# Turning on TensorE instead of by DMA, and another order in the last block of a fused transformer kernel

## The chip, the core and the metric

The kernel runs on one core of one Trainium2 chip. The metric is the device time of one execution in microseconds (us); the time before is the median of three runs, 1993.96 us (1993.28 to 1995.19). The engines of a core work side by side and meet through semaphores: TensorE (PE in the profile, with its weight loads listed as PEld), VectorE (DVE), ScalarE (ACT), GpSimd (POOL), and SyncE (SP), which issues most DMAs.

## The reference

For two sequences of 2048 tokens with 512 channels the reference computes, in float32, an attention-like block and then a feed-forward part, each added to its input:

```python
x = x + attn(cond(x, cond_512, ...), ...)     # modulated linear layer, gated linear recurrence, gated MLP
x = x + ffn(cond2(x, tokens, ...), rhs)       # the part that the change touches
```

The second line is the stage at hand. With `_ln` a layer norm over the 512 channels whose gain and shift are looked up by token class:

```python
h = _ln(x, pw_g[pathway_ids], pw_b[pathway_ids]);  h = _ln(h, cp_g[compartment_ids], cp_b[compartment_ids])
t = _ln(x, tm_g[time_steps], tm_b[time_steps]);    s = _ln(x, ms_g[scale_type], ms_b[scale_type])
m, n, r = (x + state_vector for each of three conditions)        # one vector per sequence
cat = concat([w[0]*h, w[1]*t, w[2]*m, w[3]*n, w[4]*r, w[5]*s])   # 6 x 512 channels
y = _ln(silu(cat @ int_W1 + int_b1) @ int_W2 + int_b2, int_g, int_be)
# ffn: int8-style product
q = clip(round(y / scale_y), -127, 127);  out = (q @ q_rhs) * scale_y * scale_rhs
```

`scale_y` is the largest absolute value of a token's row divided by 127, `scale_rhs` the same by column of `rhs`.

## The kernel before

**Tiling.** The first 1360 us (modulated layer, recurrence, MLP) are not touched by the change. The last stage works on 8 blocks of T = 512 tokens, 4 blocks per sequence. Within a block the channels lie on the partitions for the products, and the tokens lie on the partitions for the norms, so data must be turned between the two layouts.

**The big product.** After the terms that share `x` are merged, `cat @ int_W1` is four 512-channel operands (x, t, s, h) times a weight with 512 outputs. `up` does it with seven products in place of eight: `paired_in_place` splits operands and outputs into halves (B11, B21 are the first 256 tokens of the first and second pair of operands, B12, B22 the last 256) and runs the steps a (slot 0, B11), b (slot 1, B21), d (slot 6, B22), d (slot 4), a (slot 5), e (slot 2), a (slot 3). Each step is 16 fp32 matrix products, which the profile lists as 32 passes (L134); the letters are PSUM banks, and in the profile the tiles ps_h_a, ps_h_b, ps_h_d and ps_h_e. `tap` copies or combines what later steps need (L1576 on; L1582 is its ACT copy, tap 5 is called `less`, tap 3 is k3), `sums` forms differences of the operands in place (L222), `out11`, `out12`, `out22` and `out21` add up a quarter of the output and apply silu (L1600 to L1615), and `added` adds the parts that depend on a token's class alone by a short bf16 product with `tables` and `z2T` (L1594). `then` is a dictionary of functions that are traced after step n, or, with the key (n, u), after half u of it.

**The next block's norms.** While block i is in its steps, `by_tokens` for block i+1 turns x by TensorE (`tr_x`, L1458), takes statistics on VectorE (L1348), forms the normed rows `ln` (L1362), and prepares `z1`: one-hot rows times the norm's factors, in bf16. The turned `z1T` is the moving operand of the class gains (`gains`, L1551). `branch_by_tokens` gathers the rows of `pw` by POOL's indirect DMA (L1390), multiplies and adds them (L1502, L1503) for two pairs of token tiles, and takes the statistics of the first pair. `rows_by_tokens`, placed behind k3, takes those of the second pair and forms `z2`; its turned `z2T` serves the third gain and `added`. `branch_by_channels` turns h0 by TensorE (`tr_h`, L1371), and ACT copies it out (L1374).

**Turning by DMA.** `to_rows` (L1438) turns z1 and z2 with a transposing DMA on SP; `int8_values` (L1685) does it with the int8 values of the block before. In the first block half of z2 is turned by TensorE already (`rows_of_first`, L1529).

**The rest of a block.** `down2` multiplies by `w2` (L1633, ps_o) with the next block's gains in between, adds the bias and takes statistics. Norm, scales and int8 values of block i-1 (`last_norm`, `int8_values`) run on VectorE during block i, and `int8_product` (L1657, ps_f) on TensorE behind the product steps; VectorE scales it (L1660), adds x and SP stores it.

**The last block** has no successor. `part_norm` does the w2 product of one tile of 128 tokens, with the bias as an fp32 product of a row of ones (L1705, L1707), the norm (L1642, L1643), the scale (L1646, L1649) and the rounding (L1652); `part_product` turns by TensorE (L1725), copies on VectorE (L1727), multiplies (L1657) and stores. Tiles 2 and 3 are normed in the middle of the last step a, tiles 0 and 1 after it, and then all four products follow.

**Order of the work.** A tile framework orders each engine's instructions: by the order in which they are traced, but an instruction whose operands it estimates to be late is overtaken by later ones. `tc.issue_after(ins)` keeps what is traced in it behind `ins` on the same engine; `tc.manual_schedule` keeps the traced order (TensorE in the first block's first steps). On the chip each engine then takes its instructions in that fixed order.

**PSUM.** `m2_ps` has four buffers of one bank for products. `tr` hands out two buffers in turn (`turn[0] ^= 1`) to every turn and gain.

## Time and profile before

| what | value |
|---|---|
| time, median of 3 runs | 1993.96 us (1993.28 to 1995.19) |
| profiled execution: time, span | 1991.8 us, 1990.0 us |
| TensorE busy in the span | 1972.5 us (99%) |
| VectorE, ACT, POOL busy | 1180.4, 658.4, 146.4 us |
| granted TensorE clock, mean | 0.997 |
| last stage: one steady block | 73.03 to 73.04 us |
| last block: start to the end of its last w2 product | 1901.50 to 1973.03 us |
| from there to the end of the span | 16.97 us |

A row of a timeline gives start, duration, engine, line, operation, tiles (output <- inputs) and count; a bracket tells how long the engine stood idle before it and what released it. Tiles that share memory carry the name of the place (zone_A, zone_B, zone_C and the like): q0 is in zone_A, z1T in zone_C, and pw is the second pair's buffer. fp32 matrix products appear as two passes each. The chain of waits is followed back from the end; a row in it gives start, duration, engine, tile and line. A table of stretches gives, per engine, the busy time and number of instructions within each stretch.

### The profile page before, as it was taken

The page shows a single profiled execution, that of the slowest core. Times are in us where ns is not written, and L with a number is a line of the kernel's source. Part 1 is how long each engine was busy: PE and PEld are TensorE (multiplying, and loading weights), DVE is VectorE, ACT ScalarE, POOL GpSimd, SP SyncE. Part 2 cuts the span into 40 slices and gives each one's busy share as a digit, 9 for nine tenths or more (in the row PEclk, how much of TensorE's full clock was granted, in tenths as well). Part 3 has the DMA queues.
Part 4 walks back from the last instruction along what each step waited for, and adds up shares of the span by engine and source line. Part 5 has one row for each costly group of instructions (what it writes and reads, how often), then busy time and mean ns, then how long its engine had stood idle before and what let it go on. Part 6 is the DMA issues. An engine that isn't in the chain of part 4 may idle for free.

```text
span 1990.0 us, 16593 instructions
## 1 busy us (share of the span) xinstructions
PE 1972.5 (99%) x6060; PEld 1054.8 (53%) x6068; DVE 1180.4 (59%) x1907; ACT 658.4 (33%) x889; POOL 146.4 (7%) x123
## 2 busy tenths in 40 slices
PE   9999999999999999999999999999999999999997
PEld 5444444444444444444444444444867867877774
DVE  6667666666633324324224564646788888788775
ACT  4557777777522222222221100001213213212302
POOL 0241000000400000000010000025000000000000
PEclk9999999999999999999999999999999999999999
DMA  6661212121511212111335666453322222222110
GB/s 220 204 201 53 89 59 95 53 95 43 159 47 66 89 42 82 56 42 53 101 100 170 209 232 235 156 170 127 121 69 85 59 72 82 65 73 74 43 32 22
DMA packets 115774, 201.36 MB, mean 101 GB/s; under 512 B 37728, under 2 KB 66034, under 8 KB 111596
## 3 DMA queue, kind: packets, MB, share of 16 engines
q1 hardware_dynamic: 111028, 183.49, 28.2%
q0 software_dynamic: 4608, 16.78, 2.4%
q8 instruction: 48, 0.79, 0.2%
q14 instruction: 34, 0.28, 0.0%
q10 hardware_dynamic: 56, 0.03, 0.0%
HBM read 133.59 MB, written 58.83 MB: 97 GB/s over the span
## 4 chain that ended last, share of the span: by engine, by line
PE 93%; DVE 5%; ACT 0%; DMA 0%; issue 0%; SPq 0%; DVEq 0%
PE up_a L134 17%; PE rec_a L134 11%; PE dn_a L134 8%; PE up_d L134 8%; PE ps_h_a L134 6%; PE ps_h_d L134 6%; PE rec_d L134 6%; PE ps_o L1633 5%; PE dn_d L134 4%; PE up_b L134 4%; PE ps_h_b L134 3%; PE y_a L134 3%; PE rec_b L134 3%; PE dn_b L134 2%; PE y_d L134 1%; PE ps_f L1657 1%
## 5 line engine op out<-in xcount | busy, mean ns | idle before, releaser
L134 PE MATMUL up_a<-h,w_up 128*128 128x512 f32 x384 | 172.6, 592 | 0.0
L134 PE MATMUL dn_a<-op,w_dn 128*128 128x512 f32 x384 | 168.9, 599 | 0.0
L821 DVE SCALAR_TENSOR_TENSOR prod<-up_d,cols,k 128x512 f32<-128x512 f32 x48 | 36.0, 750 | 199.5 <-ACT k L304 199.5
L304 ACT COPY k<-up_a 128x512 f32<-128x512 f32 x144 | 84.0, 584 | 196.8 <-PE up_a L134 196.7
L801 ACT ACTIVATE gate<-gate,cols 128x512 f32<-128x512 f32 x96 | 68.8, 721 | 215.3 <-DVE gate L800 214.2
L134 PE MATMUL up_a<-h2T,w_up 128*128 128x512 f32 x288 | 129.5, 593 | 0.0
L134 PEld LDWEIGHTS up_a<-h,w_up 128*128 128x128 f32 x384 | 73.1, 190 | 91.7 <-issue 89.3
L134 PEld LDWEIGHTS dn_a<-op,w_dn 128*128 128x128 f32 x384 | 73.0, 192 | 90.2 <-issue 89.7
L134 PE MATMUL rec_a<-h,w_rec 128*128 128x512 f32 x256 | 115.1, 592 | 0.0
L134 PE MATMUL rec_a<-hT,w_rec 128*128 128x512 f32 x256 | 115.1, 592 | 0.0
L1633 PE MATMUL ps_o<-int_w,h 128*128 128x512 f32 x224 | 103.6, 606 | 0.0
L134 PEld LDWEIGHTS up_a<-h2T,w_up 128*128 128x128 f32 x288 | 54.8, 190 | 68.8 <-issue 68.8
L134 PE MATMUL up_b<-h,w_up 128*128 128x512 f32 x192 | 86.3, 592 | 0.0
L134 PE MATMUL up_d<-h,w_up 128*128 128x512 f32 x192 | 86.3, 593 | 0.0
L134 PE MATMUL dn_d<-op,w_dn 128*128 128x512 f32 x192 | 83.7, 594 | 0.0
L134 PEld LDWEIGHTS rec_a<-hT,w_rec 128*128 128x128 f32 x256 | 48.7, 190 | 61.2 <-issue 61.2
L134 PEld LDWEIGHTS rec_a<-h,w_rec 128*128 128x128 f32 x256 | 48.7, 190 | 61.2 <-issue 60.7
L304 ACT COPY k<-rec_a 128x512 f32<-128x512 f32 x96 | 55.6, 579 | 71.5 <-PE rec_a L134 70.0
L800 DVE TENSOR_TENSOR gate<-up_b,k 128x512 f32<-128x512 f32 x48 | 32.9, 690 | 72.1 <-PE up_b L134 71.0
L134 PE MATMUL up_d<-h2T,w_up 128*128 128x512 f32 x144 | 65.2, 593 | 0.0
L1633 PEld LDWEIGHTS ps_o<-int_w,h 128*128 128x128 f32 x224 | 40.3, 190 | 46.5 <-issue 46.5
L222 DVE TENSOR_TENSOR op<-op,op 128x3072 f32<-128x3072 f32 x16 | 55.2, 3448 | 16.2 <-PE dn_d L134 9.3
(408 smaller groups left out, 3403.2 us busy)
## 6 DMA issues: line engine op xcount, KB each, us to landing
pp_d<-prod SPq DMA_DIRECT2D x48, 512.0 KB
op<-pp_d SPq DMA_DIRECT2D x16, 1536.0 KB
y_d<-y SPq DMA_DIRECT2D x16, 512.0 KB
h<-y_d SPq DMA_DIRECT2D x4, 2048.0 KB
yr<-y_d SPq DMA_DIRECT2D x16, 512.0 KB
hs_d<-yr SPq DMA_DIRECT2D x16, 512.0 KB
h<-hs_d SPq DMA_DIRECT2D x4, 2048.0 KB
op<-in_xT SPq DMA_DIRECT2D x32, 256.0 KB
```

Of the source, the lines that this page charges most:

```text
L134: ins = nc.tensor.matmul(ps, ws[k // 2][:, slot, k % 2, ts(u, P)], xs[k], start=(first and k == 0), stop=(last and k == n - 1), skip_group ...
L222: nc.vector.tensor_sub(t, p, q)
L304: nc.scalar.copy(t, ps)
L800: nc.vector.tensor_add(gate[u][:, half], ps, kept)
L801: nc.scalar.activation(gate[u][:, half], gate[u][:, half], AF.Gelu, bias=col("L0_attn_mlp_gate_b", fs[u]),)
L821: nc.vector.scalar_tensor_tensor(prod[u][:, b_], ps, col("L0_attn_mlp_fc_b", fs[u]), kept, ALU.add, ALU.add)
L1633: nc.tensor.matmul(ps, h1[:, c, ts(j, P)], w2[:, c, :], start=(c == 0), stop=(c == C - 1))
L1657: nc.tensor.matmul(ps, qT[:, ts(c, P)], rq[:, c, :], start=(c == 0), stop=(c == C - 1))
```

## The change

1. **Turns.** `to_rows` no longer issues a DMA: it turns tile by tile with TensorE into a PSUM tile, and ACT copies the result out. It is called for z1 after step a (slot 5) of the block before (`then[4]`), and for z2 in `down2` behind the w2 product of tile 2. The int8 values get a function of their own, `int8_rows`, called in the middle of step n = 2 (d with slot 6, in the last block d with slot 4) and after it. In the first block both halves of z2 go through `rows_of_first`.
2. **Second pair.** The product and sum of the second pair of `branch_by_tokens` become a function `pair`, called behind `less` (`then[5]`).
3. **Last block.** With `by_tiles`, step b (B21, slot 1) comes after step e, and the last step (slot 3) is done by two tiles of 128 tokens, each followed by its sums and silu. The w2 products of tiles 2 and 3 stand in and after step b; the product of tile 2 and the w2 product of tile 0 follow the first token tile, and the others the second.
4. **Bias.** The bias row of the last block is split into three bf16 rows (`ones_b2`), made by POOL and three small DMAs at the start of the stage, and added by one bf16 product with three rows of ones.
5. **Rounding.** In the last block ACT subtracts the rounding constant, and both limits are applied where the turned tile is copied.

```diff
...
             k3 = tap(3, pa, kd)
         more(3, pd)
         out22(pd, k3)
+        if by_tiles:
+            kept = tap(7, pe, k2)
+            pb = banks("b")
+            step(pb, 1, B21, True, not added)
+            sums(B21, B21, B22)
+            c11()
+            by_tiles([x[:, k, :] for x in B21 for k in range(x.shape[1])], 3, kept)
...
+            return
         kept = [tap(6, pe, None)] if shared else []
         step(pa, 3, B21, False, not added)
         more(4, pa)
...
+    ones_b2 = io.tile([P, P + D], BF, name="ones_b2")[0:3]
+    nc.gpsimd.memset(ones_b2[:, 0:P], 1.0)
+    t = place("qT0", D)[0:1]
+    h = place("qT1", 2, D, dtype=BF)
+    nc.gpsimd.tensor_copy(t, b2_bc[0:1])
+    for n in range(3):
+        part_of = h[0:1, n % 2, :]
+        nc.gpsimd.tensor_copy(part_of, t)
+        if n < 2:
+            nc.gpsimd.tensor_sub(t, t, part_of)
+        nc.sync.dma_start(ones_b2[n : n + 1, P:], part_of)
+    less_magic = small.tile([P, 1], FP, name="less_magic", bufs=1)
+    nc.gpsimd.memset(less_magic, -MAGIC)
...
-    def to_rows(dst, src):
-        nc.sync.dma_start(
-            dst.rearrange("p a (j t) -> p (a j) t", t=P),
-            src.rearrange("p a j t -> p (a j t)"), transpose=True,
-        )
+    def to_rows(dst, src, pt):
+        for n in range(dst.shape[1]):
+            for j in range(J):
+                nc.tensor.transpose(pt[:, n, ts(j, P)], src[:, n, j, :], identb)
+        nc.scalar.copy(dst, pt)
...
         k["z1T"] = place("z1T", 2, T, dtype=BF)
-        to_rows(k["z1T"], z1)
...
                 gather(i * J + 2 * q + j, pw[:, j, :])
+        def pair(q):
             nc.vector.tensor_mul(h0[q], ln[q], h0[q])
-            nc.vector.tensor_add(h0[q], h0[q], pw[:, :, D : 2 * D])
-            if not q:
-                pair_stats(0)
+            nc.vector.tensor_add(h0[q], h0[q], place(f"pw{q}", 2, 2 * D)[:, :, D : 2 * D])
+        pair(0)
+        pair_stats(0)
+        k["pair"] = pair
         k["rest"] = z2, of_means, mv2, pair_stats
...
         k["z2T"] = place(f"z2T{i % 2}", 2, T, dtype=BF)
-        if i:
-            to_rows(k["z2T"], z2)
-        else:
-            k["z2"] = z2
-            to_rows(k["z2T"][:, 1:2], z2[:, 1:2])
+        k["z2"] = z2
         return last
-    def rows_of_first():
-        pt = m2_ps.tile([P, D], BF, tag="mm", name="tr_z2")
-        for j in range(J):
-            nc.tensor.transpose(pt[:, ts(j, P)], k["z2"][:, 0, j, :], identb)
-        nc.scalar.copy(k["z2T"][:, 0, :], pt)
+    def rows_of_first(n):
+        pt = m2_ps.tile([P, 1, D], BF, tag="mm", name=f"tr_z2_0_{n}")
+        to_rows(k["z2T"][:, n : n + 1], k["z2"][:, n : n + 1], pt)
+    def rows_of(n, i, k):
+        to_rows(k[f"z{n}T"], k[f"z{n}"], tr(f"tr_z{n}_{i}", BF))
     def by_tokens(i, k):
         norm_by_tokens(i, k)
...
         def tap(n, ps, less):
-            t = place(f"k{ {1: 0, 4: 1, 2: 2, 5: 1, 3: 1, 6: 2}[n]}", 2, H)
+            t = place(f"k{ {1: 0, 4: 1, 2: 2, 5: 1, 3: 1, 6: 2, 7: 2}[n]}", 2, H)
             if n == 5:
-                nc.vector.tensor_sub(t, ps, less)
+                held["less"] = nc.vector.tensor_sub(t, ps, less)
+            elif n == 7:
+                nc.vector.tensor_add(t, both(ps), less)
             elif n == 3:
                 held["k3"] = nc.vector.tensor_add(t, both(ps), less)
...
+            if by_tiles:
+                for o in (0, 1):
+                    silu(o, h_a, h1[:, o, h_a])
         def out12(ps, kept):
             nc.vector.tensor_add(h1[:, 0:2, h_b], both(ps), kept)
             for o in (0, 1):
-                silu(o, slice(0, T), h1[:, o, :])
+                half = h_b if by_tiles else slice(0, T)
+                silu(o, half, h1[:, o, half])
         def out22(ps, kept):
             nc.vector.tensor_add(h1[:, 2:4, h_b], both(ps), kept)
...
+        def last_by_tiles(X, slot, kept):
+            for j in (0, 1):
+                part = ts(j, P)
+                ps = [x[:, 0:P] for x in banks(f"t{j}")]
+                for u in (0, 1):
+                    product(ps[u], w_int, slot, [x[:, part] for x in X], u, not u, False)
+                added(4, ps, part)
+                for u in (0, 1):
+                    h = h1[:, 2 + u, part]
+                    nc.vector.tensor_add(h, ps[u], kept[:, u, part])
+                    silu(2 + u, part, h)
+                then["tile", j]()
+        by_tiles = last_by_tiles if i == NB - 1 else None
         paired_in_place(
             w_int, *([t[:, :, h] for t in q] for h in (h_a, h_b) for q in (first, second)),
...
                 for c in range(C):
-                    nc.tensor.matmul(
+                    ins = nc.tensor.matmul(
                         ps, h1[:, c, ts(j, P)], w2[:, c, :], start=(c == 0), stop=(c == C - 1)
                     )
+                if nxt and j == 2:
+                    with tc.issue_after(ins.ins):
+                        rows_of(2, i + 1, nxt)
                 t = o4[q][:, j % 2, :]
                 nc.vector.tensor_add(t, ps, b2_bc)
                 stats(mv, j, t, f"s3_{i}")
...
         nc.vector.tensor_scalar(qn, qn, -127.0, None, ALU.max)
-        nc.sync.dma_start(
-            place(f"qT{q}", 2, D, dtype=BF).rearrange("p j (c t) -> p (j c) t", t=P),
-            qn.rearrange("p j d -> p (j d)"), transpose=True,
-        )
+    def int8_rows(i, q, behind):
+        qn, pt = place(f"q{q}", 2, D, dtype=BF), tr(f"trq_{i}_{q}", BF)
+        with tc.issue_after(behind.ins):
+            for j in (0, 1):
+                for c in range(C):
+                    nc.tensor.transpose(pt[:, j, ts(c, P)], qn[:, j, ts(c, P)], identb)
+        nc.scalar.copy(place(f"qT{q}", 2, D, dtype=BF), pt)
     def int8_product(i, qs, x2n, q, behind):
...
         ps = m2_ps.tile([P, D], FP, tag="mm", name=f"ps_o_{i}_{j}")
-        nc.tensor.matmul(ps, ones[0:1, :], b2_bc[0:1, :], start=True, stop=False)
+        nc.tensor.matmul(ps, ones_b2[:, 0:P], ones_b2[:, P:], start=True, stop=False)
         for c in range(C):
...
         qn = places["pw0"].bitcast(BF)[:, ts(j, D)]
-        rounded(qn, t)
+        nc.scalar.activation(qn, t, AF.Identity, bias=less_magic)
         return t, qs, qn
     def part_product(i, j, t, qs, qn):
...
         qT = places["pw1"].bitcast(BF)[:, ts(j, D)]
-        nc.vector.tensor_scalar(qT, pt, -127.0, None, ALU.max)
+        nc.vector.tensor_scalar(qT, pt, 127.0, -127.0, ALU.min, ALU.max)
         by_rhs(t, qT, qs[:, 1, :], f"ps_f_{i}_{j}")
...
         norm_by_tokens(0, k, (ends[4], mids[5]))
+        rows_of(1, 0, k)
         branch_by_tokens(0, k)
+        k["pair"](1)
         branch_rows = rows_by_tokens(0, k)
...
         (0, 0, 1): times,
-        (0, 1, 1): rows_of_first,
+        (0, 1, 1): lambda: rows_of_first(0),
+        (1, 1, 0): lambda: rows_of_first(1),
         (1, 0, 0): lambda: gains(0, k, 2),
         1: first_block.close,
     }
-    def behind_k3(i, k):
-        with tc.issue_after(held["k3"].ins):
-            rows_by_tokens(i, k)
+    def behind(name, f, *args):
+        with tc.issue_after(held[name].ins):
...
             then[1] = lambda: [int8_values(i - 1, qs[0], q) for q in PAIRS]
-            then[2] = lambda: int8_product(i - 1, qs[0], last["x2n"], 0, held["ins"])
+            then[2, 0] = lambda: int8_rows(i - 1, 0, held["ins"])
+            then[2] = lambda: (
+                int8_rows(i - 1, 1, held["ins"]),
+                int8_product(i - 1, qs[0], last["x2n"], 0, held["ins"]),
+            )
             then[3, 0] = lambda: int8_product(i - 1, qs[0], last["x2n"], 1, held["ins"])
         if nxt:
             then[3] = lambda: by_tokens(i + 1, nxt)
-            then[6, 0] = lambda: behind_k3(i + 1, nxt)
+            then[5] = lambda: behind("less", nxt["pair"], 1)
+            then[6, 0] = lambda: behind("k3", rows_by_tokens, i + 1, nxt)
+            then[4] = lambda: behind("ins", rows_of, 1, i + 1, nxt)
             then[6] = lambda: branch_by_channels(i + 1, nxt)
         else:
             parts = {}
-            def half():
-                for j in (2, 3):
-                    parts[j] = part_norm(i, j)
-            then[6, 0] = half
+            def part(j):
+                parts[j] = part_norm(i, j)
+            def product_of(j):
+                part_product(i, j, *parts[j])
+            then[5, 0] = lambda: part(2)
+            then[5] = lambda: part(3)
+            then["tile", 0] = steps((product_of, 2), (part, 0))
+            then["tile", 1] = steps((product_of, 3), (part, 1), (product_of, 0), (product_of, 1))
         up(i, k, then)
         if nxt:
             down2(i, nxt)
-        else:
-            for j in (0, 1):
-                parts[j] = part_norm(i, j)
-            for j in (2, 3, 0, 1):
-                part_product(i, j, *parts[j])
         last, k = k, nxt
...
```

Step b moves likewise further up in `paired_in_place`: there `if not by_tiles` now stands ahead of its bank, its product, its sums and `c11`.

More of the change, by code (lines that the diff above doesn't have):

```diff
@@ L176, in paired_in_place @@
     def paired_in_place(ws, B11, B21, B12, B22, banks, tap, out11, out12, out21, out22,
-                        then=(), added=None, shared=False, late=None):
+                        then=(), added=None, shared=False, late=None, by_tiles=None):
         U = (0, 1)
@@ L231, in paired_in_place @@
             k1 = tap(1, pa, None)
-        pb = banks("b")
+        if not by_tiles:
+            pb = banks("b")
         if late:
@@ L237, in paired_in_place @@
             sums(B12, B22, B12)
-        if not late:
+        if not late and not by_tiles:
             step(pb, 1, B21, True, not added)
@@ L242, in c11 @@
             out11(pb, k1)
-        if not late:
+        if not late and not by_tiles:
             c11()
@@ L253, in paired_in_place @@
         step(pd, 4, B11, False, not added)
-        sums(B21, B21, B22)
+        if not by_tiles:
+            sums(B21, B21, B22)
         step(pa, 5, B22, False, False)
@@ L267, in paired_in_place @@
         out22(pd, k3)
+        if by_tiles:
+            kept = tap(7, pe, k2)
+            pb = banks("b")
+            step(pb, 1, B21, True, not added)
+            sums(B21, B21, B22)
+            c11()
+            by_tiles([x[:, k, :] for x in B21 for k in range(x.shape[1])], 3, kept)
+            return
         kept = [tap(6, pe, None)] if shared else []
@@ L1470, in norm_by_tokens @@
         k["z1T"] = place("z1T", 2, T, dtype=BF)
-        to_rows(k["z1T"], z1)
+        k["z1"] = z1
         k["ln"] = [place(f"o4_{q}", 2, D) for q in PAIRS]
@@ L1588, in silu, with added @@
             )
-        def added(n, ps):
-            o, half = {1: (0, h_a), 2: (0, h_b), 3: (2, h_b), 4: (2, h_a)}[n]
+        def added(n, ps, part=None):
+            o, half = {1: (0, h_a), 2: (0, h_b), 3: (2, h_b), 4: (2, part or h_a)}[n]
             for u in (0, 1):
@@ L1619, in up @@
             banks, tap, out11, out12, out21, out22, then, added, True, None if i else behind_branch,
+            by_tiles,
         )
@@ L1794, in adaln_attn_ffn @@
     }
-    def behind_k3(i, k):
-        with tc.issue_after(held["k3"].ins):
-            rows_by_tokens(i, k)
+    def behind(name, f, *args):
+        with tc.issue_after(held[name].ins):
+            f(*args)
     last = None
```

## The prediction

> **What bounds the kernel now.** The page comes first: it tells which engine has no room.
>
> ```profile
> PE 1972.5 (99%) x6060; PEld 1054.8 (53%) x6068; DVE 1180.4 (59%) x1907; ACT 658.4 (33%) x889; POOL 146.4 (7%) x123
> ```
>
> TensorE has work for 99% of the span, VectorE for 59%. The change lies in the last 600 us, so the next view is the busy time by stretches: one steady block, the last block up to its last product by w2, and the rest.
>
> ```profile
> core 0: us, PE busy (x) PEld busy (x) DVE busy (x) ACT busy (x) POOL busy (x), PEclk, DMA share, GB/s
> 1803.51:1876.55 73.04, 72.45 (x325) 54.47 (x325) 59.93 (x117) 16.65 (x26) 3.75 (x4) 1.00 0.23 68
> ...
> 1901.50:1973.03 71.53, 71.48 (x291) 51.52 (x292) 42.12 (x82) 11.44 (x18) 0.00 (x0) 1.00 0.08 23
> 1973.03:1990.00 16.97, 6.32 (x31) 2.16 (x29) 12.23 (x31) 0.20 (x1) 0.00 (x0) 0.76 0.17 62
> ```
>
> A block lasts 73.04 us and TensorE is busy for 72.45 of them; only in the last 16.97 us has VectorE more to do than TensorE. The table of waits then tells what TensorE's missing 0.6 us is:
>
> ```profile
> PE ps_h_d L1594 <- DVE h L1603: 3.6, 7, 0.6
> PEld ps_h_d L134 <- ACT zone_B L1582: 1.8, 7, 0.3
> ```
>
> Neither wait is for a transposing DMA. The timeline shows the first of them at its place: the product "e" ends, and the rows added to ps_h_d stand until VectorE has read ps_h_d (L1603), which it does only after both pairs of the next block's branch.
>
> ```profile
> 1873.94 1.89 PE L134 MATMUL ps_h_e<-mT,w_int 128*128 128x256 f32 x8
> 1875.64 0.66 DVE L1603 TENSOR_TENSOR h<-ps_h_d,zone_B 128x512 f32<-128x512 f32 x1
> 1876.35 0.38 PE L1594 MATMUL ps_h_d<-z2T,tables 108*128 108x256 bf16 x2 [0.51 <-DVE h L1603]
> ```
>
> The chain of waits confirms it (for 15 us of each block it runs through ACT and VectorE and comes back to TensorE right there), and shows how gains and w2 products alternate, and the end:
>
> ```profile
> 1873.31 1.14 DVE pw L1503
> 1874.44 1.20 DVE s_st L1348 x2
> 1876.73 6.91 PE ps_h_a L134 x32
> ```
>
> ```profile
> 1885.61 0.39 PE gain L1551 x2
> 1886.00 1.05 PE ps_o L1633 x2
> 1887.06 0.32 PE gain L1551 x2
> 1887.38 2.77 PE ps_o L1633 x6
> ...
> 1973.03 0.70 DVE s_st L1348
> ...
> 1986.12 0.69 DVE zone_A L1729
> ```
>
> Two rows price what is added:
>
> ```profile
> 1884.55 1.93 ACT L1374 COPY hT<-tr_h 128x1024 f32<-128x1024 f32 x2 [0.18 <-PE tr_h L1371]
> 1972.83 0.61 PE L1725 MATMUL trq<-identb,zone_B 128*128 128x128 bf16 x8
> ```
>
> **The change, part by part.**
>
> *1. Transposes on TensorE.* z1 takes 8 in each of 8 blocks (64), z2 8 in seven blocks and 4 more in the first (60), the int8 values 16 for each of 7 blocks (112): 236. Eight of the same kind took 0.61 us, the last of them 0.22, so they start (0.61 - 0.22)/7 = 0.056 us apart. 236 x 0.056 = 13.2 us; 220 of them (12.3 us) lie ahead of the last block, 16 (0.9) in it. TensorE has no free time there except its waits, so they count in full. A rule speaks harder against this part. The Trainium skill, "TensorE: Matmul & The Clock Gate", Part 4 (PE-mode transpose), puts one 128x128 bf16 transpose at about 390 ns alone and 275 ns inside a kernel. The row's single duration (0.22 us) is near that, but its pace is a quarter of it. By 275 ns each the sum here would be 65 us instead of 13.2; I go by the pace.
>
> *2. What the DMAs held.* SP issued four transposes a block; no TensorE wait names them. L1485 on ACT waited for one (12.65 us in that block), with ACT busy only 16.65 us of 73.04: nothing is gained.
>
> *3. The second pair moves behind `less`.* Its two operations (2 x 1.14 us) leave the queue ahead of L1603, which then runs some 2.3 us sooner, at about 1873.4, ahead of the end of product e. That end is its start, 1868.77, plus 32 x 0.216 = 1875.68; the rows started at 1876.35. So 0.67 us goes in each of 7 blocks: -4.7 us. What is late next: the pair now ends at about 1876.9 instead of 1874.4, so k3, out22 and the second pair's statistics wait up to 0.6 us for it; their readers (products by w2, h0's turn) come at 1883 or later. Bounds: 0 back if the wait only moves, 0.87 a block with L1582's.
>
> *4. PSUM for turning.* Two buffers serve all turns in alternation: 10 takings a block before, 14 after. In the new order z2's turn takes the buffer of the second half of the next gain, which must wait until ACT has copied z2T out: a 128x1024 copy is 1.0 us. TensorE either stands for about 1.2 us, or does w2 products between the halves, as at 1885.61 to 1887.38: there the second half cost 0.32 plus 0.19 (the six ps_o took 2.77 where 6 x 0.43 = 2.58). The row is at the same place, so I take 0.5 a block: +3.5 us. Bounds 0 and 1.2: 0 to 8.4.
>
> *5. Waits on sources.* The z1 run stands right behind product a5, which ended at 1868.77; z1 was complete at 1868.74 (L1432). I take 0; bounds 0 to 0.3 a block (2.1). The int8 values of both pairs are complete at 1843.9 and 1845.4, their turns come at about 1845.7 and 1849.3; z2 is complete at 1884.4, its turn comes near 1890. ACT's four added copies (4 x 1.0 us) fit between; were one put ahead of the copy of ps_h_d that product d4 waits for (L1582), a block would lose up to 1.0 (7 at most). I take 0, as the values' copy would end near 1851 and L1582 starts at 1851.39.
>
> *6. Bias rows, set-up.* Six POOL operations on one row and three DMAs on SP stand near 1392 to 1400. Behind them on SP are the class tables, whose last DMA was issued at 1410.13 and whose reader started at 1414.21; POOL's gathers for block 1 are read at 1431. Hidden, 0 to +3 at worst. On TensorE each of four fp32 bias products (0.86) becomes one bf16 pass (0.22): -2.6 us, inside part 7.
>
> *7. The last block.* TensorE from its start to the last product by w2: six full products 6 x 6.91 = 41.5; two token tiles of 32 passes over 128 columns. The row nearest is 38 fp32 passes of that shape (L379; twenty in 2.48 us, 0.11 to 0.12 apart): 2 x 3.6 = 7.3 with their table rows, against 6.91 for the whole. int8 product 3.5, table rows 0.65, sixteen turns 0.9; four w2 parts of 4.0 (4.68 less the 0.64): 16.1; turning and product of tiles 2 and 3, now ahead of part 1, 2 x 1.1 = 2.2. Waits: B21 no longer stands between a and d6, but d4 still needs ps_h_d copied: 0.20 + 0.59 + 0.06 = 0.85, and nothing is left to fill it, since a5's operands are behind the int8 values on VectorE; VectorE's copies of two turned tiles 0.8. Sum 73.8 against 71.5: +2.3. Then the tail. Of one tile alone, by the rows of tile 2: statistics to largest 3.9 (1955.31 to 1959.24), scale and shift 1.1, rounding on ACT instead of VectorE 0.85 (a 128x512 ACT operation 0.71, and a hand-over), turn 0.6, copy 0.5, product 1.9 at the lower clock, scale and add 1.5, store and end 3.2: 13.6; tile 0's product interleaves for some 0.7: 14.3 against 16.97: -2.7. Together -0.4. The two more silus of 128x256 (0.46 us each on ACT) and tap 7 (0.69 us on VectorE in place of an ACT copy) run while TensorE is in product b and tile 3, and cost nothing there. Bounds: -2.8 (all waits filled, no interleaving) to +6 (B21's difference, 2.4 us on VectorE, ordered behind the whole chain of tile 3).
>
> Sum: 12.3 - 4.7 + 3.5 - 0.4 = +10.7 us. The profiled execution took 1991.8 (span 1990.0 and 1.8 around it); its like would be 2002.5. The median shown stands 2.2 above it, so 1993.96 + 10.7 = 2004.7.
>
> **The rivals.** *A, cover:* the free time absorbs what it can. The switch of part 4 costs nothing, both waits go (7 x 0.87 = 6.1), the last block does its best: 12.3 - 6.1 - 2.8 = +3.4, 1997.4. For it: gains wait for nothing else. Against: the same switch costs 0.19 today at the same spot.
>
> *B, new waits:* TensorE stands for z2T's copy (8.4) and for z1 (2.1): 12.3 - 4.7 + 8.4 + 2.1 - 0.4 = +17.7, 2011.7. For it: z1 is complete only 0.03 us ahead. Against: work that can be drawn forward lies behind each.
>
> *C, faster:* the block is set not by TensorE's load but by the loop ACT, VectorE, TensorE that the chain shows from 1861 to 1876. Then turns and switches (15.8 us) are hidden, and the pair's move shortens the loop: -4.7 - 0.4 = -5.1, 1988.9. It decides only where at least 14.7 of the 15.8 are hidden, 2.1 us a block; a block has 0.59 idle. That is what speaks against it.
>
> *D:* the last block runs into part 7's upper bound: +6 in place of -0.4, 2011.1.
>
> **How the numbers follow.** A measurement tells 0.2%, 4.0 us, from no change: 1990.0 to 1998.0 is "same". My case (2000 to 2009) 0.60, A 0.17, B 0.12, C 0.05, D 0.06. Most of A and a little of mine lie within 0.2%: 0.14; C, and a trifle for what I have not seen: 0.06 faster; 0.80 slower. The range reaches from below A to above B: 1996.5 to 2012.5. Not in it are C, and B and D together.
>
> **What would show it.** Steady blocks 1.4 to 1.9 us longer, near 74.6, each with 32 bf16 transposes 0.056 us apart; the wait of L1594 for L1603 gone; gains of the second kind split by ps_o, or a wait for ACT there (B); at the end 14 us instead of 17 after the last ps_o. Wrong would be: a block no longer than 73.5 (A or C), waits at z1's or z2's turn above 0.5 us (B), over 3 us of idle TensorE between product b and the tiles (D).

## The result, and the profile after

The changed kernel takes 2008.63 us (median of four, 2007.78 to 2009.92) against 1993.62 of the kernel before (1991.53 to 1995.19): 1.0076 times as long, 95% interval 1.0059 to 1.0094, some 15 us slower. The forecast was 2004.7 us in a range of 1996.5 to 2012.5, so the sign and most of the size came out, and 4 us are missing from the sum. The profiled execution took 2009.92 us (span 2008.1), 18.1 us more than the one profiled before (1991.8). Its line of busy times:

```profile
PE 1989.2 (99%) x6325; PEld 1071.2 (53%) x6334; DVE 1182.4 (59%) x1907; ACT 695.7 (35%) x930; POOL 151.9 (8%) x131
```

TensorE has 16.7 us more work and 265 more instructions, ACT 37 us more (it now copies the turned tiles), VectorE 2 us more. The stretches that answer to those shown of before, one steady block, the last block to the end of its last w2 product, and the rest:

```profile
core 0: us, PE busy (x) PEld busy (x) DVE busy (x) ACT busy (x) POOL busy (x), PEclk, DMA share, GB/s
1842.82:1917.60 74.78, 74.70 (x357) 56.20 (x357) 59.96 (x116) 20.50 (x29) 0.00 (x0) 1.00 0.04 15
1917.60:1992.77 75.17, 71.96 (x350) 54.03 (x353) 47.03 (x94) 21.25 (x30) 0.00 (x0) 1.00 0.06 22
1992.77:2008.10 15.33, 3.75 (x16) 1.13 (x13) 7.89 (x19) 0.92 (x2) 0.00 (x0) 0.63 0.09 34
```

A block lasts 74.78 us in place of 73.03, and TensorE's idle share in it is gone (0.08 us are left). In the last block TensorE is now idle for 3.2 of 75.2 us, where it had next to no gap before (0.05), and the tail is 15.3 instead of 17.0. The table of waits of TensorE no longer has the line of L1594 (now L1623) for L1603; these stand in it instead, once each (the second to the fourth in the last block; the first in block 0, where the wait at that place was 0.4 us before). The largest wait in it, 5.3 us for ACT's rounding of the last tile, lies in the tail.

```profile
PE tr_z L1466 <- ACT q L1458: 1.6, 1, 1.6
PE ps_f L1709 <- DVE qs L1070: 1.6, 1, 1.6
...
PE ps_f L1709 <- DVE r_rv L86: 0.9, 1, 0.9
PE ps_h_d L134 <- ACT zone_B L1611: 0.7, 1, 0.7
```

The chain of waits in a steady block now stays on TensorE from one block to the next:

```profile
1809.46 0.45 PE tr_z L1466 x8
1809.91 6.96 PE ps_h_e L134 x32
1816.87 0.22 PE ps_h_d L1623 x2
...
1827.74 2.77 PE ps_o L1682 x6
1830.52 0.45 PE tr_z L1466 x8
1830.96 0.32 PE gain L1578 x2
1831.28 1.05 PE ps_o L1682 x2
1832.34 0.32 PE gain L1578 x2
```

Eight turns take 0.45 us (8 x 0.056). The rows of ps_h_d follow product e without a gap. Behind z2's turn the second gain is torn in two by two passes of a w2 product, as the first always was.

Stage by stage the two profiled executions differ by 2.1 us up to the start of ps_bias (1386.09 against 1384.03), 3.6 in the rest of block 0 (82.69 against 79.10), 6 x 1.75 = 10.5 in the steady blocks and 2.0 in the last one (90.66 against 88.66). The first figure carries little: across all profiles taken here ps_bias started anywhere from 1381.9 to 1386.3 us. That leaves two places that the sum did not foresee: block 0 and the last block.

### The profile page after: what moved, and what is told of

Same layout as the page of the kernel before. It is cut to its first block, busy times and chain, and to the rows that moved or that the text cites. A ratio compares the mean times of both kernels' runs of the same rounds, so it can differ in the third digit from the quotient of the medians.

```text
span 2008.1 us, 17088 instructions
## 1 busy us (share of the span) xinstructions
PE 1989.2 (99%) x6325; PEld 1071.2 (53%) x6334; DVE 1182.4 (59%) x1907; ACT 695.7 (35%) x930; POOL 151.9 (8%) x131
## 4 chain that ended last, share of the span: by engine, by line
PE 99%; DVE 1%; ACT 0%; issue 0%; DVEq 0%
PE up_a L134 16%; PE rec_a L134 11%; PE dn_a L134 8%; PE up_d L134 8%; PE ps_h_a L134 8%; PE ps_h_d L134 6%; PE rec_d L134 6%; PE ps_o L1682 5%; PE dn_d L134 4%; PE up_b L134 4%; PE ps_h_b L134 3%; PE ps_h_e L134 3%; PE y_a L134 3%; PE rec_b L134 3%; PE dn_b L134 2%; PE ps_f L1709 1%
```

## The experiments

The stage times below come from each run's profile: "block 0" runs from ps_bias to block 1's first product, "last block" from its first product to the end. The runs were made on three chips; the ratios are against runs of the kernel before on the same chip, whose medians there were 1992.83, 1993.61 and 1993.40 us.

**The parts one by one.** First the pair alone, on the kernel before.

```diff
+            then[5] = lambda: behind("less", nxt["pair"], 1)
-            then[6, 0] = lambda: behind_k3(i + 1, nxt)
+            then[6, 0] = lambda: behind("k3", rows_by_tokens, i + 1, nxt)
```

> Only the move of the second pair behind `less`, on the kernel before. Theory (step 3 of the prediction): the wait of L1594 for L1603 goes in seven blocks at 0.67 us each, -4.7 us, so about 1989, with steady blocks of 72.36 us in place of 73.03. Rival 1: the wait only moves to a later place (k3, the second pair's statistics or h0's turn), 0 us, so about 1993.6. Rival 2: the later pair makes its readers late by more than it frees, +1 to +4 us.

1989.53 us against 1992.83 (ratio 0.9988, 0.9979 to 0.9997). Steady blocks take 72.62 us: 0.41 less, not 0.67. The table of waits of this kernel names the rest:

```profile
PE gain L1555 <- ACT hT L1374: 1.9, 7, 0.3
```

The wait of the rows for VectorE is gone, and 0.27 us in each of seven blocks come back where the first gain waits for ACT to copy the turned h0. That copy stands in ACT's queue behind the copy of z2's rows (1517.49 in block 1), which waits for the second pair's statistics and factors on VectorE. Counted from the start of block 1, these come hardly sooner than before (the copy at 55.45 us in place of 55.58), while TensorE turns h0 0.67 us sooner (54.50 in place of 55.17). The prediction had looked at what the later pair makes late and put it at nothing; it had not looked at what now has to come sooner. 0.41 + 0.27 make up the 0.67 that was there.

Then the turns alone, again on the kernel before, with the DMAs replaced for z1, z2 and the int8 values.

```diff
+    def rows_of(n, i, k):
+        to_rows(k[f"z{n}T"], k[f"z{n}"], tr(f"tr_z{n}_{i}", BF))
...
+            then[2, 0] = lambda: int8_rows(i - 1, 0, held["ins"])
...
+            then[4] = lambda: behind("ins", rows_of, 1, i + 1, nxt)
```

> Only the turns on TensorE (z1, z2 and the int8 values) in place of the transposing DMAs, on the kernel before. Theory (steps 1 and 4): 236 turns at 0.056 us are 13.2 us, the split of a gain by w2 products 0.5 us in seven blocks is 3.5 us; +16.7 us, about 2010, and steady blocks near 75.2 us (73.03 + 1.35 + 0.5 + what the kept wait adds). The late z2 of block 0 may add 1 us. Rival 1 (C of the prediction): the block is set by the loop over ACT and VectorE, so the turns are covered; at most +2 us, about 1995. Rival 2: the turns are cheap and the whole loss of the change lies in the last block and the bias set-up; +5 us at most.

2008.36 us (ratio 1.0074, 1.0060 to 1.0088): 15.5 us more: the turns alone make the size of the whole change. A steady block takes 74.94 us, 1.91 more. Its chain of waits shows what becomes of the rows' wait when the pair is not moved:

```profile
1883.29 0.45 PE tr_z L1440 x8
1883.73 6.96 PE ps_h_e L134 x32
1890.69 0.01 issue
1890.70 0.38 PE ps_h_d L1591 x2
```

The rows take 0.38 in place of 0.22: of the 0.67 us, 0.16 are left. VectorE's read of ps_h_d (L1600 there) still ends last, at 1890.66. z1's turn stands ahead of product e and shifts the rows by 0.45, which is time in which VectorE catches up. So 0.51 us of turning is covered here, and the split of the second gain (its price follows below) gives the same back. The move of the pair is worth 0.41 a block without the turns but only 0.16 with them (74.94 to 74.78).

The last block's order, the bias rows with their set-up, and the rounding on ACT, alone:

```diff
+            then[5, 0] = lambda: part(2)
+            then[5] = lambda: part(3)
+            then["tile", 0] = steps((product_of, 2), (part, 0))
+            then["tile", 1] = steps((product_of, 3), (part, 1), (product_of, 0), (product_of, 1))
...
+    ones_b2 = io.tile([P, P + D], BF, name="ones_b2")[0:3]
```

> Only the last block's new order with its token tiles, the bf16 bias rows (set-up included) and the rounding on ACT, on the kernel before. Theory as predicted (step 7 without the 0.9 us of turns, step 6 at nothing): -1.3 us, about 1992.3. Theory as the trace of after now reads: the last block is longer by 2.0 - 0.9 = 1.1 us, and the set-up stretches VectorE's operations in block 0, by 1.5 to 2.6 us on TensorE; +2.6 to +3.7 us, about 1996.8. Rival: the set-up is hidden, and the late block 0 of after came from the turns there; +1.1 us, about 1994.7.

1996.38 us (ratio 1.0016, 1.0007 to 1.0025), 3.5 more: as the trace of the changed kernel was read, not as predicted. The steady blocks are unchanged (73.03), the last block is longer by 0.7 (89.37), and block 0 by 3.0 (82.13).

And the whole change without the turns:

```diff
-    def to_rows(dst, src, pt):
+    def to_rows(dst, src):
+        nc.sync.dma_start(
+            dst.rearrange("p a (j t) -> p (a j) t", t=P),
+            src.rearrange("p a j t -> p (a j t)"), transpose=True,
+        )
```

> The whole change but with the transposing DMAs kept in place of the turns on TensorE. Theory: the turns with their PSUM buffers carry the loss (16.7 us and more), the rest is -4.7 for the pair and +2.6 to +3.7 for the last block and the set-up; about 1992, that is some 17 us below the changed kernel. Rival: the parts do not add, since the turns fill a wait that stays without them; then it is within 10 us of the changed kernel, 1999 or more.

1993.18 us (ratio 1.0005, 0.9996 to 1.0014), 15.5 below the changed kernel. The parts add: -3.3 for the pair, +15.5 for the turns, +3.5 for the rest are +15.7, and the whole is +15.0. That is luck in part. Beside the turns the pair brings some 1.8 us less over seven blocks (0.16 in place of 0.41 in each), and a spell of TensorE at half its clock, worth 1.7 us (see block 0 below), stands in the profile of the turns alone and in that of the last block alone, but only once in that of the whole change. The two nearly cancel.

**What a turn costs.** The changed kernel with every one of the 236 turns issued twice:

```diff
-        for n in range(dst.shape[1]):
+        for n in (*range(dst.shape[1]), *range(dst.shape[1])):
...
-            for j in (0, 1):
+            for j in (0, 1, 0, 1):
```

> The changed kernel with each of the 236 turns issued twice in a row, the second time with the same operands into the same place; the output is the same. Theory (step 1 of the prediction): a turn costs its pace, 0.056 us, wherever it stands, since TensorE has no free time: 13.2 us more, about 2021.8, steady blocks longer by 32 x 0.056 = 1.8, near 76.57 us. Rival 1: part of the turns falls into TensorE's waits (for z2, for copies): under 10 us. Rival 2: the longer runs make the gains wait for ACT's copies as well: 16 us or more. The Trainium skill, TensorE: Matmul & The Clock Gate, Part 4, gives 275 ns for a transpose inside a kernel; by that it would be 65 us.

2020.46 us (ratio 1.0136, 1.0121 to 1.0152), 11.8 above the changed kernel. The steady blocks are the sharper measure: 76.56 in place of 74.78, 1.78 for 32 turns, 0.056 each. (236 such turns are 13.2 us, 1.4 more than the medians differ by; the profile of this kernel lacks the spell at half clock, 1.7 us, that the changed kernel's has in block 0, see below.) A timeline shows sixteen in a row and the next product 0.89 us after their start:

```profile
1893.38 1.06 PE L1466 MATMUL tr_z<-identb,zone_A 128*128 128x128 bf16 x16
1894.27 1.95 PE L134 MATMUL ps_h_e<-zone_A,w_int 128*128 128x256 f32 x8
```

The pace from the eight turns of the old kernel carried over. By the Trainium skill's figure of 275 ns inside a kernel ("TensorE: Matmul & The Clock Gate", Part 4: PE-mode transpose) the estimate would have been 65 us; the measurement decides against it for turns in a row. The same page's Part 1, "Wait — 56ns, not 53.3ns?", gives 55.6 ns from start to start for a matmul of 128 columns at the full clock, and that agrees with the 0.056.

**PSUM for turning.** The changed kernel with z2's turn in one of the four product buffers:

```diff
+        pt = tr(f"tr_z{n}_{i}", BF) if n == 1 else m2_ps.tile(
+            [P, 2, D], BF, tag="mm", name=f"tr_z{n}_{i}"
+        )
+        to_rows(k[f"z{n}T"], k[f"z{n}"], pt)
-        to_rows(k[f"z{n}T"], k[f"z{n}"], tr(f"tr_z{n}_{i}", BF))
```

> The changed kernel, but z2's turn takes one of the four PSUM buffers of the products in place of one of the two for turning. Theory (step 4 of the prediction): the second half of the next gain no longer waits for ACT's copy, it stands again beside the first, and the split (predicted 0.5 us a block, 0.36 by the steady blocks: 74.78 - 72.62 less four turn runs of 0.45) goes; -2.5 to -3.5 us, about 2005.6, steady blocks near 74.4. Rival: the split is what w2 products fill anyway, so at most the second pass of a gain (0.13 us a block) goes: -0.9 us at most, about 2007.7; or the first product of the next block now waits for its buffer, and nothing is gained or up to 3 us are lost.

2005.72 us (ratio 1.0059, 1.0044 to 1.0075), 2.9 less, and steady blocks of 74.26 us, 0.51 less. The gain is in one piece again in the chain of waits:

```profile
1826.69 0.45 PE tr_z L1466 x8
1827.14 0.33 PE gain L1581 x4
1827.47 3.63 PE ps_o L1685 x8
```

0.33 + 3.63 stand where 0.32 + 1.05 + 0.32 + 2.77 stood. The product buffer is free in time; no new wait appears.

**Block 0.** In the changed kernel VectorE and POOL work side by side on small operations there. The timeline of both:

```profile
1394.74 1.15 POOL L1355 TENSOR_TENSOR qT<-qT,qT 1x512 f32<-1x512 f32 x1
...
1395.05 0.88 DVE L1381 TENSOR_SCALAR r_rv<-mv 128x4 f32<-128x4 f32 x1
...
1397.73 1.14 POOL L1355 TENSOR_TENSOR qT<-qT,qT 1x512 f32<-1x512 f32 x1
...
1397.85 1.06 DVE L1425 COPY w_v<-r_rstd 128x4 f32<-128x4 f32 x1
...
1399.98 0.60 POOL L1353 CAST qT<-qT 1x512 bf16<-1x512 f32 x1
1400.12 0.82 DVE L1449 TENSOR_TENSOR q<-onehot,w_rows 128x120 bf16<-128x120 bf16 x2
```

In the trace of before the same three took 0.17, 0.17 and 0.50 us:

```profile
1394.52 0.17 DVE L1355 TENSOR_SCALAR r_rv<-mv 128x4 f32<-128x4 f32 x1
...
1396.10 0.17 DVE L1399 COPY w_v<-r_rstd 128x4 f32<-128x4 f32 x1
...
1397.52 0.50 DVE L1423 TENSOR_TENSOR q<-onehot,w_rows 128x120 bf16<-128x120 bf16 x2
```

Each stretched one starts while POOL has one row in hand, and the two single ones end a little after POOL's. Together they take 1.9 us longer, but the first of them delays nothing: ACT, which takes its result next, is busy with the copies of h0 until 1396.9. z2's turn starts 15.30 us after ps_bias, 0.9 later than before (14.44), and TensorE waits for it. So the set-up was moved to the last block, where POOL has nothing else to do:

```diff
+            then[3] = lambda: behind("ins", bias_rows)
```

> The changed kernel, but POOL prepares the bf16 bias rows in the last block instead of in block 0. Theory 1: POOL's six operations in block 0 stretched VectorE's small ones (0.88, 1.06 and 0.82 us where 0.17, 0.17 and 0.50 are usual: 1.9 us), and TensorE, idle for longer, then ran at half its clock for some 3 us (1.5 us lost); the operations are short again, block 0 falls from 82.7 us to between 79.4 and 81.0, and the time by 1.7 to 3.3 us, to about 2006. Theory 2: the turns alone make block 0 that long (with them alone, without any set-up on POOL, it took 82.66 us): the operations are short again but block 0 stays within 0.5 us, about 2008.6. In the last block POOL has nothing else to do, so 0 there; at worst part 2 waits up to 3 us for the rows.

> The transposing DMAs, the moved pair and the new last block, with the bias rows prepared in the last block. Theory: against the same kernel with the set-up in block 0 (1993.2 us, block 0 of 81.47 us) the 2.8 us that the set-up cost there come back: block 0 near 78.7, about 1990.4. Rival: the set-up was not what made block 0 longer (TensorE's order was), and the time stays at 1993.

Without the turns the move is clear: 1989.71 us (ratio 0.9983, 0.9974 to 0.9992) against 1993.18 (ratio 1.0005) with the set-up in block 0; block 0 falls from 81.47 to 78.94 us, about the length that it has without any set-up (78.70 with the pair alone). With the turns the median hardly moves, 2008.40 (ratio 1.0075, 1.0059 to 1.0090), although z2's turn starts at 14.37 us again and block 0 in the profile falls from 82.69 to 80.91. This execution was the shortest of its four (2006.39; the others 2008.19 to 2009.65), and the reason is in a comparison with the turns alone, where block 0 took 82.66 without any set-up. TensorE's timeline in that kernel (turns alone):

```profile
1398.68 0.38 PE L1440 MATMUL tr_z<-identb,q 128*128 128x128 bf16 x4 [0.64 <-ACT q L1432]
1399.98 1.13 PE L134 MATMUL ps_h_b<-tT,w_int 128*128 128x256 f32 x4 [0.92 <-DVE tT L1552]
1401.71 2.07 PE L134 MATMUL ps_h_b<-tT,w_int 128*128 128x256 f32 x4 [0.60 <-DVE tT L1552]
```

and in the one with the set-up moved:

```profile
1398.71 0.38 PE L1468 MATMUL tr_z<-identb,q 128*128 128x128 bf16 x4 [0.66 <-issue]
1400.01 1.13 PE L134 MATMUL ps_h_b<-tT,w_int 128*128 128x256 f32 x4 [0.92 <-DVE tT L1584]
1401.74 1.13 PE L134 MATMUL ps_h_b<-tT,w_int 128*128 128x256 f32 x4 [0.60 <-DVE tT L1584]
```

The same three waits to within 0.02 us, but the same four passes take 2.07 us in the first and 1.13 in the second. (The third wait is new in both: before, four passes of ps_h_d stood at that place.) The busy time by half-microseconds in the first shows why (the third figure from the right is the granted clock):

```profile
1401.50:1402.00 0.50, 0.29 (x1) 0.29 (x2) 0.16 (x1) 0.00 (x0) 0.00 (x0) 0.67 1.05 387
1402.00:1402.50 0.50, 0.50 (x2) 0.41 (x2) 0.00 (x0) 0.00 (x0) 0.00 (x0) 0.50 1.01 375
...
1405.00:1405.50 0.50, 0.50 (x4) 0.45 (x3) 0.50 (x1) 0.00 (x0) 0.00 (x0) 0.92 0.24 82
```

TensorE ran at half its clock from about 1401.67 to 1405.08 (a mean of 0.67 and one of 0.92 in the outer stretches give 0.33 and 0.08 us at half), 3.4 us, which costs 1.7. In the kernel with the set-up moved the granted clock is 1.00 throughout block 0:

```profile
1402.00:1404.00 2.00, 2.00 (x12) 1.31 (x12) 0.77 (x1) 0.62 (x1) 0.00 (x0) 1.00 0.95 384
```

In the profile of the changed kernel the same spell lies at 1402.76 to 1406.18. It is also in the profiles of the last block alone, of the whole change without the turns, and of the one with z2's turn in a product buffer, all with the set-up in block 0 and a wait of 1.6 to 1.9 us for z2; so 1.7 of the 2.5 to 3.0 us that the set-up costs there without the turns are this spell. With every turn doubled there was none, though TensorE waited longer, and none in the seven profiles with neither the turns nor that set-up. So these waits make the spell possible, and whether it comes differs from profile to profile; what decides it is not shown. That the three unprofiled executions of the kernel with the set-up moved had it, and so were some 2 us longer, fits but was not seen.

**The last block.** The bf16 bias rows by themselves, with the pair moved and the old order of the last block:

```diff
-        nc.tensor.matmul(ps, ones[0:1, :], b2_bc[0:1, :], start=True, stop=False)
+        nc.tensor.matmul(ps, ones_b2[:, 0:P], ones_b2[:, P:], start=True, stop=False)
...
+            then[3] = lambda: behind("ins", bias_rows)
```

> The kernel before, with the pair moved, and with bf16 bias rows prepared in the last block; its last block is otherwise the old one. Theory: against the pair alone (1989.5) four products of 0.86 us become four of 0.22 on TensorE's path: -2.6 us, about 1987, faster than both kernels. Rival 1: parts 2 and 3 stand where TensorE would wait anyway, so half or less: 1988.3 or more. Rival 2: POOL's operations in the last block stretch VectorE's ahead of the parts: 1989.5 or more.

1988.07 us (ratio 0.9972, 0.9961 to 0.9984). The stretches of the last block and its tail, first with the pair alone, then with the bias rows as well:

```profile
1897.77:1969.43 71.66, 71.66 (x292) 51.57 (x291) 42.10 (x82) 11.43 (x18) 0.00 (x0) 1.00 0.08 23
1969.43:1987.20 17.77, 7.11 (x32) 2.48 (x29) 12.21 (x31) 0.20 (x1) 0.00 (x0) 0.73 0.16 59
```

```profile
1897.66:1966.39 68.73, 68.68 (x288) 50.77 (x287) 40.72 (x77) 11.44 (x18) 0.00 (x0) 1.00 0.08 24
1966.39:1985.60 19.21, 6.93 (x31) 2.69 (x29) 13.07 (x36) 0.20 (x1) 0.00 (x0) 0.69 0.14 55
```

TensorE is done 2.9 us sooner, and the tail grows by 1.4: VectorE, which has 13 us of work in it, does not come along. Half of the gain stays.

This kernel also prices the new order. With the new order and ACT's rounding as well, and all else alike (transposing DMAs, pair moved, set-up late), the last block takes 89.65 us, and with the old order 87.94: the new order costs some 1.7 us. From kernel to kernel the last block reads 88.66 before, 89.43 with the pair, 87.94 with the bias rows added, 89.65 with the new order added and 90.70 with the turns added. The first of these steps is in the tail alone (17.0, 17.8 with the pair, 17.5 with the turns alone); why is open, and it tells how far such a difference can be trusted.

From the kernel without turns and with the late set-up (last block 89.65: 74.38 to the last w2 product, 15.27 after it) two single edits follow. Tile 3's product behind the last w2 product:

```diff
-            then["tile", 1] = steps((product_of, 3), (part, 1), (product_of, 0), (product_of, 1))
+            then["tile", 1] = steps((part, 1), (product_of, 3), (product_of, 0), (product_of, 1))
```

> The kernel with transposing DMAs, moved pair, new last block and late bias rows (1989.7 us; last block 89.65, of them 74.38 to the last product by w2 and 15.27 after it), with one thing changed: the turning and product of tile 3 are put behind the last w2 product instead of ahead of it. Theory: TensorE stood 1.57 us there for VectorE's copy of the turned tile, and the turning and product take another 1.0; so the last w2 product ends some 2.6 us sooner, near 71.8, and the tail grows by 1.5 to 2, since tile 3's scale and add (1.43 us) now come between the operations of the last tile: 0.6 to 1.1 us sooner in all, last block near 88.8. Rival: the tail is VectorE's and gives all of it back or more: last block 89.6 to 90.5.

1988.73 us (ratio 0.9978, 0.9969 to 0.9988). In the profile the last w2 product ends after 72.27 us (2.1 sooner), the tail is 16.06 (0.8 longer), the block 88.33: 1.3 less, by the stages. The medians, from different chips, differ by 1.0, less than they can tell apart.

And VectorE's scale and add of tile 0 held behind the last tile's scaling:

```diff
+        def late():
+            return tc.issue_after(held["scaled"].ins) if j in (0,) else nullcontext()
...
+        with late():
+            nc.vector.tensor_add(t, t, place(f"x2n{i % 2}", J, D)[:, j, :])
```

> The same kernel as the one before in this call sets out from (last block 89.65, tail 15.27), with VectorE's scale and add of tile 0 (0.75 and 0.69 us) held behind the scaling of the last tile. Theory: in the tail these two stand in the middle of the last tile's chain and delay it by 1.3 to 1.9 us, where the prediction put 0.7; held, they fit into the 1.5 us that VectorE waits for ACT's rounding and the turn: tail 13.4 to 14.0. Rival: the chain only waits elsewhere (for the clock of TensorE, for the store): tail above 14.8.

The tail falls to 13.48 us, 1.8 less, and the last block to 87.87. VectorE's timeline shows the two (L1713, L1786) in the gap before the last copy:

```profile
1979.90 0.49 DVE L1701 TENSOR_SCALAR zone_A<-zone_A,qs 128x512 f32<-128x512 f32 x1
1980.30 0.75 DVE L1713 SCALAR_TENSOR_TENSOR zone_A<-ps_f,qs,rsbc 128x512 f32<-128x512 f32 x1
1981.08 0.69 DVE L1786 TENSOR_TENSOR zone_A<-zone_A,x2n 128x512 f32<-128x512 f32 x1
1981.84 0.42 DVE L1780 TENSOR_SCALAR pw<-trq 128x512 bf16<-128x512 bf16 x1
```

The median, 1989.51 us (ratio 0.9981, 0.9971 to 0.9990), does not show it against the 1989.71 of the kernel it sets out from, measured on another chip: what lies ahead of the stage was 3 us later in this profile (ps_bias at 1386.3 against 1383.2), and such shifts are as large as the effect. It is shown by the stages alone.

The same idea on the kernel with the old last block, for tile 3:

```diff
+            return tc.issue_after(held["scaled"].ins) if j in (3,) else nullcontext()
```

> The fastest kernel so far (moved pair, bf16 bias rows prepared in the last block, old order of the last block: 1988.1 us, tail 19.21), with VectorE's scale and add of tile 3 held behind the rounding of the last tile. Theory: VectorE works without a gap for 10 us of that tail, so 1.43 us less ahead of the last tile's turning ends it sooner by 0.8 to 1.4, since 1.65 us of VectorE's wait lie behind: tail near 18.0, about 1987. Rival: the two then delay the products of tiles 0 and 1 by as much: tail 19 or more, 1988.

1987.00 us (ratio 0.9968, 0.9956 to 0.9981), tail 18.15 in place of 19.21. This is the lowest median here, 6.4 us below the kernel before and 21.6 below the changed one; the kernel that it sets out from (1988.07) is not told apart from it by the medians.

## Why the prediction was right, and where its sum was short

The signs that the prediction named came mostly true: steady blocks of 74.78 (1.4 to 1.9 longer, near 74.6), the wait of the rows gone, the second gain split by ps_o; but the tail is 15.3 and not 14. Of the two profiled executions, 18.1 us apart, the sum is short by 2.6 us in block 0, 2.4 in the last block and 0.8 in the six steady blocks; the other 1.6 lie ahead of ps_bias, where profiles scatter by more. The medians miss 4.3 us, less than the 5.8 of the stages: the spell at half clock need not be in every execution.

- **Step 1, turns (13.2 us): right.** Doubling gives 0.056 us each.
- **Step 2, the DMAs held nothing: right.** The sum of a steady block closes (below) with no gain from them.
- **Step 3, the pair (-4.7): right in the sum, by luck in part.** The wait of 0.67 is gone in the changed kernel. Alone the move brings 0.41 a block (the gains then wait 0.27 for ACT's copy of h0, which stands behind z2's rows; the prediction had put what comes next at nothing); beside the turns it brings 0.16, since z1's turn fills 0.45 of that wait anyway. In the prediction both were counted in full, the turn as a cost and the wait as a gain, and for the two together that is the right total: 0.51 filled and 0.16 saved.
- **Step 4, PSUM for turning (0.5 a block): right, 0.51.** The row of before at the same place was the right row. Steps 1, 3 and 4 make 1.78 - 0.67 + 0.51 = 1.62 for a steady block (the prediction had 1.62); 1.75 was measured. Of the 0.13 left, some 0.05 each stand at two of the four runs of turns, whose next product takes 6.96 in place of 6.91 and 3.51 in place of 3.46.
- **Step 5, waits on sources (0): right in the steady blocks, wrong in block 0.** Of the waits that the turns brought, one was overlooked: with the turns alone, TensorE waits 0.60 more for VectorE's second tT in block 0, since four passes of ps_h_d that filled that time now come later.
- **Step 6, set-up of the bias rows ("hidden, 0 to +3 at worst"): wrong, at its bound.** Without the turns it makes block 0 longer by 2.5 to 3.0 us, 1.7 of it by the spell at half clock. The prediction looked only for readers of the rows and for queues behind them on SP and POOL. It missed that VectorE's operations grew longer while POOL worked, and that TensorE, waiting longer, lost its clock.
- **Steps 5 and 6 together:** block 0 took 3.6 us more: 20 turns are 1.1, the split of a gain 0.5, the later z2 0.9 and the spell at half clock 1.7, less some 0.7 for the rows' wait that is gone. The prediction's sum had about 1.0 for that block.
- **Step 7, the last block (-0.4): wrong, +2.0, mechanism right and two terms too small.** The wait for kd (0.85 predicted, 0.7), the token tiles (3.6 each, 3.57) and the parts fit. VectorE's copies of two turned tiles were put at 0.8 us of TensorE's time; they cost 0.9 + 1.6, since on VectorE the second stands behind the sums of the second token tile (L1660) and the row maximum of tile 0 (L1698). And tile 0's product was to delay the last tile's chain by 0.7; holding it back brings 1.8. The two are 1.7 and 1.1 more than predicted, 0.4 over the 2.4 us that were missed; smaller terms came out below the sum. The chain of waits of the changed kernel shows the second, with tile 0's product and its scale and add (L1712, L1786) between the last tile's small operations:

```profile
1993.88 1.05 PE ps_f L1709 x4
...
1995.03 0.75 DVE zone_A L1712
1995.78 0.07 DVE r_rstd L1383
1995.85 0.66 DVE zone_A L1786
1996.50 0.08 DVE r_rv L86
```

Rival C, the loop over ACT and VectorE as the bound, falls with the turns alone: 1.91 us more a block, where it allowed next to nothing. A (cover) falls with it, since step 4's split is real. B fails at z1 and at z2T, where TensorE does not wait. D had the right place and the right sign, but the last block lost a third of what it said (2.0 of 6), and not for B21's difference: TensorE did not wait for that.

## What to carry over

TensorE was busy for 99% of the span, and work moved onto it was paid in full, however small the pieces, while time freed elsewhere (the DMA share of a block fell from 0.23 to 0.04) was worth nothing. Of the parts of this change the moved pair and the bf16 bias rows saved time, the turns and the new order cost it. A wait that disappears and work that is put ahead of it compete for the same time, so their gains and costs are added for the pair of them and not each alone. In a tail that is one dependent chain, look at which operations of finished tiles the scheduler slips into it: holding back two operations of 0.7 us each, the first of which waited for its product, shortened it by 1.8 us.

## What the runs showed of the hardware

- **VectorE's small operations stretched while POOL worked in SBUF.** Operations of 0.17 us took 0.88 and 1.06, each beginning within POOL's operation on a single row of 512 and ending 0.04 us behind it, and a pair of 0.50 took 0.82; with the set-up moved away the same took 0.17, 0.31 and 0.50. The Trainium skill, "SBUF — State Buffer", Who interferes with whom, has a shared pair of ports that only one of the two engines holds at a time; a VectorE copy, cast or tensor_scalar can take it, and an operation with two inputs in SBUF contends there with a POOL operation that reads SBUF. The kinds of the stretched ones fit. Two statistics of VectorE beside POOL's first copies were not stretched (1.29 us together, as before).
- **TensorE's clock fell to half for 3.4 us after waits of 0.64, 0.92 and 0.60 us within 4 us, in the profile of one kernel and not in that of another with the same waits.** Five profiles have the spell, at 3.41 to 3.42 us each: this one and four of the five with a wait of 1.6 us or more for z2. The same skill's "TensorE: Matmul & The Clock Gate", Part 1, What's actually happening, tells of a window of 3413 ns that runs freely of the kernel, which fits both the length and the chance. It puts the fall after an idle window of that length; here no single wait reached 1 us in the kernel with the turns alone, so shorter waits close together were enough.
- **What lies ahead of the changed stage varies by 4 us from execution to execution** (ps_bias from 1381.9 to 1386.3), which is more than most of the effects measured here. Steady blocks repeat to 0.03 us where nothing differs, block 0 to 0.3 (78.62 to 78.94 in three kernels alike up to there); they carry what medians cannot.
